# Layer 0's x read a second time, laid out by feature, and normalised with statistics sent through memory

## The chip, the cores and the metric

The kernel runs on one core of one Trainium2 chip. The metric is device microseconds of one execution. Three runs of the kernel before took 1642.39, 1643.19 and 1645.04 us, so the median is 1643.19 us.

The engines go by their short names: PE is TensorE, PEld its weight load, DVE is VectorE, ACT is ScalarE, POOL is GpSimd, SP is SyncE. SP computes nothing here; it issues DMAs, strictly in the order of its queue.

## The reference

Two transformer layers on `x` of 2 x 2048 tokens with 512 features, f32 throughout:

```python
x = x + L0_xattn(layernorm(x), ctx, ctx, pad, ...)   # 16 heads of 64, RoPE, tanh cap at 30, causal, own layer norm (g, b) inside
x = x + L0_ffn(layernorm(x), ...)                    # fake-quantised SwiGLU, 1408 wide
x = x + L1_xattn(layernorm(x), ctx, ctx, mask, ...)  # 16 heads of 32, biases
x = x + L1_ffn(layernorm(x), ...)                    # top-1 of 8 experts
```

The change touches the first line and the keys and values of the third. In the first line the query input is a layer norm of a layer norm: `q = layer_norm(layernorm(x), g, b) @ Wq`. For each token a mean and one combined factor (the power -1/2 of `var*(1+EPS) + EPS*EPS`) are enough, followed by a scale `g` and a shift `b` for each feature. In the third line the context `ctx` (2 x 128 x 512) is multiplied by `Wk` and `Wv` without a norm.

## The kernel before, in words

**Residency.** `x` stays in SBUF as 32 tiles `xs[n]` of 128 tokens x 512 features, tokens on the partitions. A matmul on PE contracts over partitions, so the query projection needs x by feature (features on partitions): `xnT[k]`, 128 x 4 x 256.

**Layer 0's attention** works in 16 blocks `k` of 256 tokens (two tiles; batch alternates from block to block), and in each block on 4 groups `g` of 4 heads. A unit is `u = 4k + g`; there are 64. The order of PE, DVE and ACT is written out by hand in a loop over `u` (with `tc.manual_schedule`). POOL's and SP's orders are not written out: a scheduler places their instructions. An iteration of the loop does, on PE in this order:

- `scores(u)`: keys times queries, 16 matmuls (`sc<-q`), then ACT takes a tanh and an exponential of them;
- `queries(u + 2, 0)`: 8 matmuls (`pq<-xnT,wq`), of which DVE makes two rope products `rt[0]`, `rt[1]`;
- `mixed(u - 1)`: probabilities times values (`sc<-pr`), then DVE's reciprocal (L410) and weighting `att` (L411);
- `queries(u + 2, 1)`: 8 more matmuls, products `rt[2]`, `rt[3]` on DVE, and POOL joins them to `q` (L372, L374). So a `q` is made two units ahead of the `scores` that read it. There is one set of `rt` buffers, so the next unit's first products wait for POOL to have read the last ones;
- `projected(u - 2, t)`: 8 matmuls into `pw`.

Two things more hang on the group number.

- **The norm.** At `g == 2` of block k, `normed(k + 2)` takes the statistics of block k+2's two tiles on DVE (`variance`, `ve`) and the power on POOL (L327, `rr`); `centered(k + 2)` then subtracts the mean and multiplies by the factor on DVE (L103, `xn<-x,mv,rr`, tokens on partitions, so both are per-partition scalars). At the end of iterations `g == 0` and `g == 1`, `turned(k + 1, c0)` turns half of the block each: 4 PE transposes (L345, `pt<-ident,xn`) and 2 ACT instructions that apply `g` and `b` while they copy from PSUM into `xnT` (L347). `queries` of the next block read `xnT` from `g == 2` on.
- **The weights of the FFN.** At `g == 0` and `g == 3` a weight slice `w_in` is quantised on DVE (L271 to L277) and sent through a DMA transpose; the next slice is loaded meanwhile (`w_in` has 2 buffers).

Block 0 is normed and turned ahead of the loop, among the keys and values of the context; block 1 is centered there and turned at u = 0 and u = 1. In the blocks 0 and 1 POOL also applies the causal mask to the probabilities (L392).

**Start.** SP issues all loads in one order: weights of the keys, two tiles of x, weights of the values and queries, two tiles of x, rope tables, `wo` (2 MB), the rest of x. The last 23 tiles of x (`homes`) hold weights and context first, and are loaded when these have been read.

**Layer 1's keys** come after layer 0's attention. The context is loaded by token (`cx0`, `cx1`, on ACT's queue), turned on PE (8 transposes, `pt<-ident,cx`), copied by ACT into `ctxT` (L624), and `keys(f)` multiply it (L628). Beside them DVE finishes the last block and finds the largest |x|, which PE turns (`pm`, L590); from it comes the quantisation step of the FFN.

**Memory round trip that is there already.** `v_dram` is written by one DMA (L700) and read back, sent to all partitions, into `rowadd`; POOL then adds it to `wgate` (L703).

Of the kernel before, what the change touches and what calls it, by code (L numbers as in the profile page):

```python
# [11 lines left out]
F32 = mybir.dt.float32  # L12
# [5 lines left out]
AF = mybir.ActivationFunctionType  # L18
ALU = mybir.AluOpType
# [4 lines left out]
P = 128  # L24
B, S, T, D = 2, 2048, 128, 512
ND = D // P
# [27 lines left out]
B0 = 256  # L54
NB0 = B0 // P
# [7 lines left out]
def two_layers(ctx: ExitStack, tc: tile.TileContext, a, out):  # L63
    nc = tc.nc
# [5 lines left out]
    small = ctx.enter_context(tc.tile_pool(name="small", bufs=4))  # L70
    dram = ctx.enter_context(tc.tile_pool(name="dram", bufs=1, space=DRAM))

    def load(dst, src):
        nc.sync.dma_start(out=dst, in_=src)
# [11 lines left out]
    xs = [x[:, :D] for x in xw]  # L86
# [15 lines left out]
    def center(dst, x, mean, scale):  # L102
        nc.vector.tensor_scalar(dst, x, mean, scale, ALU.subtract, ALU.mult)  # L103
# [7 lines left out]
    def transposed(psum, src, n=ND):  # L111

        pt = psum.tile([P, n, P], F32, name="pt", tag="m")
        for c in range(n):
            nc.tensor.transpose(pt[:, c, :], src[:, c * P : (c + 1) * P], ident)
        return pt
# [33 lines left out]
    with ExitStack() as l0:  # L150
# [40 lines left out]
                wk[g].append(w.rearrange("p (c o f) -> p c o f", c=2, o=2))  # L191
        for n in order[:NB0]:
            load(xs[n], x_in[n])
        for c in range(ND):
            wv.append([])
            for f in range(E0 // D):
                w = xs[homes[8 + 2 * c + f]]
                load(w, a["L0_xattn_Wv"][c * P : (c + 1) * P, f * D : (f + 1) * D])
                wv[c].append(w)
# [6 lines left out]
        def tables_in(j):  # L206
            tabs[j] = []
            for name in ("rope_cos", "rope_sin"):
                tab = mid.tile([P, B0], F32, name=name)
                load(tab, a[name][:, j * B0 : (j + 1) * B0])  # L210
                tabs[j].append(tab)

        tables_in(0)
        load(wo, a["L0_xattn_Wo"].rearrange("(c p) f -> p c f", p=P))
        for n in order[2 * NB0 : -23]:
            load(xs[n], x_in[n])
# [62 lines left out]


        def gate_up_in(name, i):
            w = wtmp.tile([P, D], F32, name="w_in", tag="w_in")
            load(w, a[name][i * P : (i + 1) * P, :])
            return w

# [26 lines left out]
        blocks = [(j, b) for j in range(S // B0) for b in range(B)]  # L312
        tiles = [[b * TPB + j * NB0 + t for t in range(NB0)] for j, b in blocks]
        nu = len(blocks) * NG
        norms, xns, xnTs, ropes, qs, prs, atts, pws = {}, {}, {}, {}, {}, {}, {}, {}

        sc = pss.tile([P, 4, 512], F32, name="sc")

        def normed(k):


            for t, n in enumerate(tiles[k]):
                mv = variance(xs[n])
                ve = small.tile([P, 1], F32, name="ve")
                nc.vector.tensor_scalar(ve, mv[:, 1:2], 1.0 + EPS, EPS * EPS, ALU.mult, ALU.add)
                rr = small.tile([P, 1], F32, name="rr")
                nc.gpsimd.tensor_tensor(rr, ve, minus_half, ALU.pow)  # L327
                norms[k, t] = mv, rr

        def centered(k):  # L330
            xns[k] = []
            for t, n in enumerate(tiles[k]):
                mv, rr = norms[k, t]
                xn = mid.tile([P, D], F32, name="xn")
                center(xn, xs[n], mv[:, 0:1], rr)
                xns[k].append(xn)

        def turned(k, c0):

            if c0 == 0:  # L340
                xnTs[k] = mid.tile([P, ND, B0], F32, name="xnT")
            pt = psm.tile([P, 2, B0], F32, name="pt", tag="m")
            for c in range(2):
                for t, xn in enumerate(xns[k]):
                    nc.tensor.transpose(pt[:, c, t * P : (t + 1) * P], xn[:, (c0 + c) * P : (c0 + c + 1) * P], ident)  # L345
            for c in range(2):
                nc.scalar.activation(  # L347
                    xnTs[k][:, c0 + c, :], pt[:, c, :], AF.Identity,
                    bias=lnb[:, c0 + c : c0 + c + 1], scale=lng[:, c0 + c : c0 + c + 1],
                )  # L350

        def queries(u, par):
# [86 lines left out]
        def steps_along(j):  # L439

            dg = wtmp.tile([P, P], F32, name="dg", bufs=1)
            nc.vector.tensor_scalar(dg, ident, sd[:, j : j + 1], None, ALU.mult)

            def rest():
                pd = psm.tile([P, P], F32, name="pdg", tag="m")
                nc.tensor.matmul(pd, ones, dg, start=True, stop=True)
                nc.scalar.copy(sdb[:, j * P : (j + 1) * P], pd)

            return rest
# [6 lines left out]
        with tc.manual_schedule(engines={E.PE, E.DVE, E.Activation}):  # L456
            context()
            for g in range(NG):
                keys(g)
                if g == 1:  # L460
                    normed(0)
                if g == 2:
                    centered(0)
            nc.vector.tensor_scalar(pad, padu, -1e30, None, ALU.mult)
            for c in range(0, ND, 2):
                turned(0, c)
            values(0, 0)
            values(0, 1)
            queries(0, 0)
            values(1, 0)  # L470
            normed(1)
            queries(0, 1)
            values(1, 1)
            for n in homes:
                load(xs[n], x_in[n])
            queries(1, 0)
            centered(1)
            queries(1, 1)
            for u in range(nu + 2):
                k, g = divmod(u, NG)  # L480
                if u < nu:
                    scores(u)
                if u + 2 < nu:
                    queries(u + 2, 0)
                elif 1 < u < nu:
                    projected(u - 2, 0)
                if 0 < u <= nu:
                    mixed(u - 1)
                if u + 2 < nu:
                    queries(u + 2, 1)  # L490
                if u > 1:
                    for t in range(0 if u + 2 < nu or u >= nu else 1, NB0):
                        projected(u - 2, t)
                if g < 2 and k + 1 < nblk:
                    turned(k + 1, 2 * g)
                if u in turns:
                    turns[u]()
                if u in diags:
                    diags[u]()
                if g == 1 and k > 0:  # L500
                    for t in range(NB0):
                        finished(k - 1, t)
                    largest(k - 1, 0)
                if g == 2:
                    if k > 0:
                        largest(k - 1, 1)
                    if k + 2 < nblk:
                        normed(k + 2)
                        centered(k + 2)
                if g in (0, NG - 1) and u > 1:  # L510
                    if makes and not loaded:
                        load_, args, _, _ = makes[0]
                        loaded.append(load_(*args))
                    elif makes:
                        _, _, make, args = makes.pop(0)
                        turns[u + 1] = make(loaded.pop(), *args)
                        if makes:
                            load_, args, _, _ = makes[0]
                            loaded.append(load_(*args))
                if nu - 5 <= u < nu - 1:  # L520
                    diags[u + 1] = steps_along(u - nu + 5)
                if u == NG:
                    for name, clip in clips.items():
                        kept[name] = const.tile([P, 1], F32, name=f"kept_{name}")
                        nc.scalar.activation(kept[name], clip, AF.Exp, scale=-1.0)
                        nc.vector.tensor_scalar(kept[name], kept[name], 1.0, None, ALU.add)
                        nc.vector.reciprocal(kept[name], kept[name])
                if u == nu - 2:
                    load(wk1, a["L1_xattn_WkT"].rearrange("(c p) f -> p c f", p=P))
                    load(wv1, a["L1_xattn_WvT"].rearrange("(c p) f -> p c f", p=P))  # L530
            largest(nblk - 1, 1)
# [67 lines left out]
    with ExitStack() as up:  # L599
# [3 lines left out]
        kv = up.enter_context(tc.tile_pool(name="kv1", bufs=1, reuse_waits="tile"))  # L603

        ctxT = kv.tile([P, ND, B * T], F32, name="ctxT")
        cxs = [kv.tile([P, D], F32, name=f"cx{b}") for b in range(B)]
        bk = kv.tile([P, ND], F32, name="bk")
        bvb = kv.tile([P, D], F32, name="bvb")

        for b in range(B):  # L610
            nc.scalar.dma_start(out=cxs[b], in_=a["ctx_1024"][b])
        nc.scalar.dma_start(out=bk, in_=a["L1_xattn_bk"].rearrange("(c p) -> p c", p=P))
        load(bvb, a["L1_xattn_bv"].partition_broadcast(P))
        load(wq1, a["L1_xattn_WqT"].rearrange("(c p) f -> p c f", p=P))
# [4 lines left out]
        load(masks, a["mask_scores"].rearrange("(j p) k -> p j k", p=P))  # L619


        for b in range(B):
            pt = transposed(psm, cxs[b])
            nc.scalar.copy(ctxT[:, :, b * T : (b + 1) * T], pt)  # L624
        def keys(f):
            pk = psm.tile([P, B * T], F32, name="pk", tag="m")
            for c in range(ND):
# [656 lines left out]
```

## Time and profile before

| | us |
|---|---|
| median of 3 runs | 1643.19 (1642.39 to 1645.04) |
| the profiled execution: its own time | 1642.48 |
| its span in the profile | 1640.8 |
| PE busy | 1597.7 (97%) |
| DVE busy | 1185.9 (72%) |
| ACT busy | 686.3 (42%) |
| POOL busy | 437.5 (27%) |

The granted PE clock is 0.998 over the span. A row of the groups has the line, engine, operation, written and read tiles, shape and count; then busy time, mean duration of one in ns, idle time of the engine ahead of it and what ended that. In a timeline a row is a run of like instructions: start, duration in us, what, and in brackets the idle time before it. In the table of windows each engine has its busy time in us and its count of instructions, and the last three columns are the granted clock, the share of time that the DMA engines were busy, and GB/s. The page's chain of work that ended last holds only the last 8 us of this kernel, and so says nothing of layer 0; the windows and the timelines do.

### The profile page before, as it was taken

To read this page: it belongs to the slowest core of one execution; us is meant where nothing else is said; L and a number is where in the kernel's file an instruction comes from. 1 tells how busy PE (TensorE), PEld (TensorE's weight loads), DVE (VectorE), ACT (ScalarE), POOL (GpSimd) and SP (SyncE) were. 2 spreads that over 40 slices of the span, in tenths; PEclk is the share of its full clock that TensorE was granted. 3 is DMA by queue.
4 is the path that set the end of the run, shared out by engine and by line. 5 is a ranking of instruction groups with operands and counts; after the bars stand their busy time and mean duration, and the time that the engine had idled before them with its cause. 6 is when DMAs were issued, how large, how long until landed. Compare 5 with 4: busy or idle time off the path is not lost. (4 is left out here: it accounts for less than half of the span.)

```text
span 1640.8 us, 26515 instructions
## 1 busy us (share of the span) xinstructions
PE 1597.7 (97%) x9962; PEld 952.5 (58%) x9962; DVE 1185.9 (72%) x2290; ACT 686.3 (42%) x1539; POOL 437.5 (27%) x498
## 2 busy tenths in 40 slices
PE   7999999999999999989999999999999999999997
PEld 5666666665666666534443566666666666654543
DVE  3466666777777765689986678898999889876332
ACT  1222222222222222234436576666666665662332
POOL 2322222222222221110005632333333221224553
PEclk9999999999999999999999999999999999999999
DMA  9400111010100220556658650001000000113332
GB/s 318 151 17 22 28 26 27 20 27 20 27 20 14 54 37 1 161 161 183 186 175 294 235 204 16 27 20 33 21 27 20 21 14 21 40 47 103 125 124 67
DMA packets 123883, 128.61 MB, mean 78 GB/s; under 512 B 43857, under 2 KB 91433, under 8 KB 123756
## 3 DMA queue, kind: packets, MB, share of 16 engines
q1 hardware_dynamic: 114508, 107.03, 21.2%
q0 software_dynamic: 6240, 18.70, 3.6%
q8 instruction: 80, 1.31, 0.3%
q10 hardware_dynamic: 3008, 1.19, 0.3%
q14 instruction: 47, 0.39, 0.1%
HBM read 78.96 MB, written 41.76 MB: 74 GB/s over the span
## 5 line engine op out<-in xcount | busy, mean ns | idle before, releaser
L362 PE MATMUL pq<-xnT,wq 128*128 128x256 f32 x1024 | 254.4, 392 | 0.0
L420 PE MATMUL pw<-wo,att 128*128 128x512 f32 x512 | 230.9, 593 | 0.0
L362 PEld LDWEIGHTS pq<-xnT,wq 128*128 128x128 f32 x1024 | 184.6, 190 | 66.9 <-issue 46.7
L855 ACT ACTIVATE s<-s,mx 128x128 f32<-128x128 f32 x512 | 176.7, 387 | 18.1 <-DVE mx L846 18.1
L388 ACT ACTIVATE pr<-sc 128x1024 f32<-128x1024 f32 x64 | 65.5, 1024 | 237.8 <-PE sc L383 234.7
L372 POOL TENSOR_TENSOR q<-rt,rt 128x256 f32<-128x256 f32 x64 | 46.5, 726 | 410.5 <-DVE rt L371 410.5
L420 PEld LDWEIGHTS pw<-wo,att 128*128 128x128 f32 x512 | 97.0, 190 | 96.2 <-issue 89.8
L410 DVE RECIPROCAL rd<-sc 128x256 f32<-128x256 f32 x64 | 112.5, 1757 | 51.1 <-PE sc L404 51.1
L1119 PE MATMUL pz<-we,x 128*128 x312 | 140.7, 594 | 0.6 <-issue 0.5
L813 PE MATMUL pq<-xT,wq 128*128 128x256 f32 x512 | 124.1, 385 | 0.0
L347 ACT ACTIVATE xnT<-pt,lnb,lng 128x256 f32<-128x256 f32 x64 | 32.6, 559 | 216.1 <-PE pt L345 216.1
L367 DVE TENSOR_TENSOR rt<-pq,rope_cos 128x256 f32<-128x256 f32 x64 | 27.2, 425 | 130.8 <-PE pq L362 120.2
L905 PE MATMUL pw<-wo,oT 128*128 128x512 f32 x256 | 115.5, 594 | 1.6 <-DVE oT L897 1.6
L928 PE MATMUL pl<-wgate,xnT 128*128 128x512 f32 x256 | 115.1, 592 | 0.0
L813 PEld LDWEIGHTS pq<-xT,wq 128*128 128x128 f32 x512 | 94.9, 190 | 28.0 <-issue 13.6
L716 ACT ACTIVATE gate<-pg,gsc 128x512 f32<-128x512 f32 x88 | 60.5, 687 | 96.5 <-PE pg L711 85.8
L711 PE MATMUL pu<-xqT,wuT 128*128 128x512 bf16 x352 | 90.3, 379 | 5.3 <-DVE h L719 5.3
L91 DVE BATCH_NORM_STATS2 st<-x 128x6 f32<-128x512 f32 x130 | 89.6, 689 | 5.6 <-DMA x<-in_ctx 3.4
L841 DVE SCALAR_TENSOR_TENSOR s<-sc,keep 128x1024 f32<-128x1024 f32 x64 | 77.9, 1217 | 20.6 <-PE sc L833 20.6
L1123 DVE TENSOR_TENSOR x<-x,x 128x512 f32<-128x512 f32 x39 | 27.0, 692 | 90.0 <-ACT x L1122 89.8
L711 PE MATMUL pg<-xqT,wgT 128*128 128x512 bf16 x352 | 90.3, 379 | 0.0
L1119 PEld LDWEIGHTS pz<-we,x 128*128 128x128 f32 x312 | 56.4, 190 | 58.2 <-issue 57.9
(218 smaller groups left out, 2847.7 us busy)
## 6 DMA issues: line engine op xcount, KB each, us to landing
h_dram<-h SPq DMA_DIRECT2D x88, 256.0 KB
hq<-h_dram SPq DMA_DIRECT2D x31, 704.0 KB
x_dram<-x SPq DMA_DIRECT2D x32, 258.0 KB
x<-in_x SPq DMA_DIRECT2D x32, 256.0 KB
we<-in_L_ffn_We SPq DMA_DIRECT2D x8, 1024.0 KB
w_in<-in_L_ffn_w_gate SPq DMA_DIRECT2D x11, 256.0 KB
w_down<-in_L_ffn_w_down SPq DMA_DIRECT2D x4, 704.0 KB
w_in<-in_L_ffn_w_up SPq DMA_DIRECT2D x11, 256.0 KB
```

Of the source, the lines that this page charges most:

```text
L91: nc.vector.bn_stats(out=st, in_=x)
L362: nc.tensor.matmul(pq, wqs[c // 2][:, c % 2, par, g * P : (g + 1) * P], xnTs[k][:, c, :], start=(c == 0), stop=(c == ND - 1))
L388: nc.scalar.activation(pr, sc[:, :, :B0], AF.Tanh, scale=1.0 / (math.sqrt(DH0) * GROK))
L410: nc.vector.reciprocal(rd, sc[:, 0, B0:])
L420: nc.tensor.matmul(pw, atts[u][:, f, t * P : (t + 1) * P], wo[:, 2 * g + f, :], start=(g == 0 and f == 0), stop=(g == NG - 1 and f == 1),)
L711: nc.tensor.matmul(dst, w[:, c, i * P : (i + 1) * P], xqTs[blk][:, c, :], start=(c == 0), stop=(c == ND - 1),)
L813: nc.tensor.matmul(pq, wq1[:, c, f * P : (f + 1) * P], xTs[blk][:, c, :], start=(c == 0), stop=(c == ND - 1))
L841: nc.vector.scalar_tensor_tensor(s, sc[:, 2 * half : 2 * half + 2].rearrange("p r c k -> p (r c) k"), -MASKED, keeps[n].unsqueeze(1).to_br ...
L855: nc.scalar.activation(s[:, h, :], s[:, h, :], AF.Exp, bias=mx[:, h : h + 1], **accum)
L905: nc.tensor.matmul(pw, os_[n][:, c, :], wo1[:, c, :], start=(c == 0), stop=(c == ND - 1))
L928: nc.tensor.matmul(pl, xn2T[n][:, c, :], wgate[:, c, :], start=(c == 0), stop=(c == ND - 1))
L1119: nc.tensor.matmul(pz, ring[j][:, c, :], we[:, bass.ds(e, 1), c, :], start=(c == 0), stop=(c == ND - 1))
```

## The change

The host sends two more arrays: `x_turned`, x by feature in blocks of 256 tokens, and `ctx_turned`, the context by feature. For blocks 1 to 15 `xnT[k]` is loaded directly (512 KB, `features_in`). Its mean and factor now vary along the free dimension, so each block's statistics (`stat`, 128 x 2 x 2) go by a DMA to DRAM in pieces of 4 bytes, come back by a second DMA that sends the row of 512 numbers to all partitions (`along`), and two tensor-tensor instructions of 128 x 1024 apply them: the subtraction on POOL (`centered`), the product on DVE (`scaled`). ACT then applies `g` and `b` in place (`affine`). `normed(k + 2)` sends at `g == 2` of block k; `centered` and `scaled` of that block stand at `g == 0` of block k+1, two units later; all four `affine` instructions at `g == 1`. Block 0 goes the old way (`first_block`). `xnT` has 3 buffers instead of 2, `along` one, `w_in` one instead of two. The per-token `x` is still loaded, for the residual and the statistics.

```diff
+        def features_in(k):
+            xnTs[k] = mid.tile([P, ND, B0], F32, name="xnT", bufs=3)
+            load(xnTs[k], a["x_turned"][k // B, k % B])
...
         tables_in(0)
+        features_in(1)
         load(wo, a["L0_xattn_Wo"].rearrange("(c p) f -> p c f", p=P))
...
-            w = wtmp.tile([P, D], F32, name="w_in", tag="w_in")
+            w = wtmp.tile([P, D], F32, name="w_in", tag="w_in", bufs=1)
...
         def normed(k):
+            stats[k] = small.tile([P, NB0, 2], F32, name="stat")
             for t, n in enumerate(tiles[k]):
...
-                rr = small.tile([P, 1], F32, name="rr")
-                nc.gpsimd.tensor_tensor(rr, ve, minus_half, ALU.pow)
-                norms[k, t] = mv, rr
+                nc.vector.tensor_copy(stats[k][:, t, 0:1], mv[:, 0:1])
+                nc.gpsimd.tensor_tensor(stats[k][:, t, 1:2], ve, minus_half, ALU.pow)
+            if k > 1:
+                features_in(k)
+            if k > 0:
+                turned_in(k)
+
+        def turned_in(k):
+            nc.sync.dma_start(out=stat_dram[k].rearrange("t s p -> p (t s)"), in_=stats[k].rearrange("p t s -> p (t s)"))
+            along[k] = mid.tile([P, NB0, 2, P], F32, name="along", bufs=1)
+            load(along[k], stat_dram[k].partition_broadcast(P))
+
+        def by_token(k, i, op, engine):
+            x = xnTs[k].rearrange("p c (t q) -> p c t q", t=NB0)
+            engine.tensor_tensor(x, x, along[k][:, :, i].unsqueeze(1).to_broadcast([P, ND, NB0, P]), op)
 
         def centered(k):
...
+            by_token(k, 0, ALU.subtract, nc.gpsimd)
+
+        def scaled(k):
+            by_token(k, 1, ALU.mult, nc.vector)
...
+        def affine(k, c0, pt=None):
+            for c in range(c0, c0 + 2):
                 nc.scalar.activation(
-                    xnTs[k][:, c0 + c, :], pt[:, c, :], AF.Identity,
+                    xnTs[k][:, c, :], xnTs[k][:, c, :] if pt is None else pt[:, c - c0, :], AF.Identity, bias=lnb[:, c : c + 1], scale=lng[:, c : c + 1]
                 )
...
                 if u < nu:
                     scores(u)
+                if g == 0 and k + 1 < nblk:
+                    centered(k + 1)
...
-                if g < 2 and k + 1 < nblk:
-                    turned(k + 1, 2 * g)
+                if g == 1 and k + 1 < nblk:
+                    for c in range(0, ND, 2):
+                        affine(k + 1, c)
...
                         normed(k + 2)
-                        centered(k + 2)
...
+                if g == 0 and k + 1 < nblk:
+                    scaled(k + 1)
...
-        for b in range(B):
-            nc.scalar.dma_start(out=cxs[b], in_=a["ctx_1024"][b])
+        nc.scalar.dma_start(out=ctxT, in_=a["ctx_turned"])
...
-        for b in range(B):
-            pt = transposed(psm, cxs[b])
-            nc.scalar.copy(ctxT[:, :, b * T : (b + 1) * T], pt)
```

In the built program the changed parts stand so on the queues that the scheduler fills. On SP, for each block in the middle of the stage: the load of `xnT` of block k+1, the write of block k's `stat`, the load of its `along`, then `w_in` and the DMA transpose of the group's weights, twice. On POOL, for each block: the two powers of `normed`, straight after them `centered` of the same block (not two units later, where the loop calls it), and then the `q` of `g == 3`, `g == 0` and `g == 1`. The first product of the following unit on DVE (`rt[0]`) now waits for POOL. In block 0 one mask (that of u = 3) stands behind `centered(2)`. At the start `stat(1)` is written between the loads of the `homes` on SP, with three more loads between it and `along(1)`.

More of the change, by code (lines that the diff above doesn't have):

```diff
@@ L193, in two_layers @@
             load(xs[n], x_in[n])
+        xnTs = {}
+        def features_in(k):
+            xnTs[k] = mid.tile([P, ND, B0], F32, name="xnT", bufs=3)
+            load(xnTs[k], a["x_turned"][k // B, k % B])
         for c in range(ND):
@@ L314, in two_layers @@
         nu = len(blocks) * NG
-        norms, xns, xnTs, ropes, qs, prs, atts, pws = {}, {}, {}, {}, {}, {}, {}, {}
+        stats, along, ropes, qs, prs, atts, pws = {}, {}, {}, {}, {}, {}, {}
+        stat_dram = dram.tile([len(blocks), NB0, 2, P], F32, name="stat_dram")
         sc = pss.tile([P, 4, 512], F32, name="sc")
         def normed(k):
+            stats[k] = small.tile([P, NB0, 2], F32, name="stat")
             for t, n in enumerate(tiles[k]):
@@ L325, in normed @@
                 nc.vector.tensor_scalar(ve, mv[:, 1:2], 1.0 + EPS, EPS * EPS, ALU.mult, ALU.add)
-                rr = small.tile([P, 1], F32, name="rr")
-                nc.gpsimd.tensor_tensor(rr, ve, minus_half, ALU.pow)
-                norms[k, t] = mv, rr
-        def centered(k):
[L331 to L346, printed above, removed]
+                nc.vector.tensor_copy(stats[k][:, t, 0:1], mv[:, 0:1])
+                nc.gpsimd.tensor_tensor(stats[k][:, t, 1:2], ve, minus_half, ALU.pow)
@@ new lines, in centered, with first_block, rest @@
+        def centered(k):
+            by_token(k, 0, ALU.subtract, nc.gpsimd)
+        def scaled(k):
+            by_token(k, 1, ALU.mult, nc.vector)
+        def first_block():
+            xn = mid.tile([P, NB0, D], F32, name="xn", tag="xnT", bufs=3)
+            for t, n in enumerate(tiles[0]):
+                center(xn[:, t, :], xs[n], stats[0][:, t, 0:1], stats[0][:, t, 1:2])
+            xnTs[0] = mid.tile([P, ND, B0], F32, name="xnT", bufs=3)
+            def rest():
+                for c0 in range(0, ND, 2):
+                    pt = psm.tile([P, 2, B0], F32, name="pt", tag="m")
+                    for c in range(2):
+                        for t in range(NB0):
+                            nc.tensor.transpose(
+                                pt[:, c, t * P : (t + 1) * P], xn[:, t, (c0 + c) * P : (c0 + c + 1) * P], ident
+                            )
+                    affine(0, c0, pt)
+            return rest
@@ L347, in turned @@
+        def affine(k, c0, pt=None):
+            for c in range(c0, c0 + 2):
                 nc.scalar.activation(
-                    xnTs[k][:, c0 + c, :], pt[:, c, :], AF.Identity,
-                    bias=lnb[:, c0 + c : c0 + c + 1], scale=lng[:, c0 + c : c0 + c + 1],
+                    xnTs[k][:, c, :], xnTs[k][:, c, :] if pt is None else pt[:, c - c0, :], AF.Identity, bias=lnb[:, c : c + 1], scale=lng[:, c : c + 1]
                 )
@@ L462, in two_layers @@
                 if g == 2:
-                    centered(0)
+                    first = first_block()
             nc.vector.tensor_scalar(pad, padu, -1e30, None, ALU.mult)
-            for c in range(0, ND, 2):
-                turned(0, c)
+            first()
             values(0, 0)
@@ L476, in two_layers @@
             queries(1, 0)
-            centered(1)
             queries(1, 1)
@@ L605, in two_layers @@
         ctxT = kv.tile([P, ND, B * T], F32, name="ctxT")
-        cxs = [kv.tile([P, D], F32, name=f"cx{b}") for b in range(B)]
         bk = kv.tile([P, ND], F32, name="bk")
         bvb = kv.tile([P, D], F32, name="bvb")
-        for b in range(B):
-            nc.scalar.dma_start(out=cxs[b], in_=a["ctx_1024"][b])
+        nc.scalar.dma_start(out=ctxT, in_=a["ctx_turned"])
         nc.scalar.dma_start(out=bk, in_=a["L1_xattn_bk"].rearrange("(c p) -> p c", p=P))
@@ L1254 @@
     arrays["mask_pad"] = arrays.pop("mask_BxS2_bf0")
+    arrays["x_turned"] = arrays["x"].reshape(B, S // B0, B0, ND, P).transpose(1, 0, 4, 3, 2)
+    arrays["ctx_turned"] = arrays["ctx_1024"].reshape(B * T, ND, P).transpose(2, 1, 0)
     arrays["mask_scores"] = arrays.pop("mask_1x1xSxS2_bk0").reshape(S, T)
```

## Prediction

> **What bounds the kernel now.** I read the table of windows first, because the change lies in layer 0 and a share over the whole span hides a stage. Columns: window, us, then PE, PEld, DVE, ACT, POOL busy with counts, granted clock, DMA share, GB/s.
>
> ```profile
> 0.00:41.00 41.00, 31.00 (x111) 22.48 (x112) 16.28 (x49) 5.99 (x11) 9.31 (x19) 1.00 0.90 318
> 287.00:369.00 82.00, 82.00 (x541) 50.13 (x538) 57.93 (x113) 21.46 (x24) 16.98 (x24) 1.00 0.11 23
> ```
>
> The start is bound by loads (DMA 0.90, PE 31 of 41 us). After that PE is busy without a gap; DVE has 58 of 82 us, POOL 17, DMA 0.11. The list of waits says the same: from 60 to 656 us PE waited once, for 0.4 us. So what leaves PE's queue here shortens the kernel, as long as nothing else becomes later than PE.
>
> Next, PE's timeline over one block (units of `g` = 2, 3, 0, 1 start at 303.03, 312.82, 322.61, 332.83; the next at 343.06):
>
> ```profile
> 303.03 0.71 PE L383 MATMUL sc<-q,kTe 32*128 32x256 f32 x8
> ...
> 312.82 0.71 PE L383 MATMUL sc<-q,kTe 32*128 32x256 f32 x8
> ...
> 322.61 0.71 PE L383 MATMUL sc<-q,kTe 32*128 32x256 f32 x8
> ...
> 332.30 0.60 PE L345 MATMUL pt<-ident,xn 128*128 128x128 f32 x4
> 332.83 0.71 PE L383 MATMUL sc<-q,kTe 32*128 32x256 f32 x8
> ...
> 342.53 0.60 PE L345 MATMUL pt<-ident,xn 128*128 128x128 f32 x4
> 343.06 0.71 PE L383 MATMUL sc<-q,kTe 32*128 32x256 f32 x8
> ```
>
> Units without transposes last 9.79 us twice, those with them 10.22 and 10.23. The price of four transposes is this difference, 0.43 to 0.44 us, not four times their duration of 273 ns: they overlap.
>
> Then POOL and DVE around the place where the new wait comes (a row's bracket is the idle time before it):
>
> ```profile
> 314.44 0.79 POOL L327 TENSOR_TENSOR rr<-ve,minus_half 128x1 f32<-128x1 f32 x1 [0.46 <-DVE ve L325]
> 320.41 0.73 POOL L372 TENSOR_TENSOR q<-rt,rt 128x256 f32<-128x256 f32 x1 [5.18 <-DVE rt L371]
> 321.10 0.72 POOL L374 TENSOR_TENSOR q<-rt,rt 128x256 f32<-128x256 f32 x1
> ```
> ```profile
> 325.79 0.42 DVE L367 TENSOR_TENSOR rt<-pq,rope_cos 128x256 f32<-128x256 f32 x1 [3.21 <-PE pq L362]
> 326.13 0.41 DVE L368 TENSOR_TENSOR rt<-pq,rope_sin 128x256 f32<-128x256 f32 x1
> 327.25 1.76 DVE L410 RECIPROCAL rd<-sc 128x256 f32<-128x256 f32 x1 [0.70 <-PE sc L404]
> 329.04 0.69 DVE L411 TENSOR_TENSOR att<-sc,rd 128x512 f32<-128x512 f32 x1
> ```
>
> POOL has 5.2 us free after the power and DVE 3.2 us before its next product.
>
> **Part 1, transposes of layer 0.** 15 blocks lose two groups of four: 15 x (10.22 + 10.23 - 2 x 9.79) = 15 x 0.87 = 13.05 us. One group gives nothing: at u = 1 no projection covers DVE, and PE waits for `att` after the transposes.
>
> ```profile
> 62.83 0.71 PE L383 MATMUL sc<-q,kTe 32*128 32x256 f32 x8 [0.41 <-DVE att L411]
> ```
>
> Take 0.43 off: **-12.6 us**.
>
> **Part 2, what DVE, ACT and POOL get instead** (all beside PE, priced at nothing while the cover holds). DVE loses two `xn` of 0.54 and 0.55 us and a wait of 0.44 behind `normed`, and gains two copies of 0.15 (as L430) and one tensor-tensor of 1024: 256 elements take 0.41, 512 take 0.69, so about 1.25. That last one stands after the quantisation of `g == 0`, which ends at 332.36, and DVE is then idle 3.66 us until 336.01: it fits with 2.4 us over. ACT's four instructions of 0.56 us move to `g == 1`, behind the exponential that ends at 336.25: done by 338.5, while `queries` read `xnT` after 344. The subtraction on POOL: 256 elements take 0.73 us and 512 take 1.27 (L1204) with little beside, or a median of 1.85 beside a busy DVE (L780). Extended to 1024 that is 2.4 or 4.1 us; I take 2.7, since DVE is half idle there. `w_in` with one buffer: its load is issued when the quantisation has read the slice (322.57) instead of at 323.85 behind the DMA transpose; the bytes of such a load had moved by 326.5, and DVE wants them at 330.31. No cost: if the load took 4 us longer, the quantisation would begin late and run into DVE's 3.66 us of idle time.
>
> The GPSIMD Engine Reference of the Trainium skill (4.1, Engine selection) speaks against the subtraction on POOL: two-input elementwise work belongs on VectorE, GpSimd being about twice as slow. The rows agree on the ratio (1.27 to 0.69 us), but on DVE it would add 1.25 us to the nearly same idle stretch; by rule or by row the sum stays the same.
>
> **Part 3, the round trip, and who waits behind it.** The built order puts the subtraction straight behind the powers on POOL, so POOL waits there for `along`, and behind it stand `q` (L372, L374), behind these DVE's next `rt`, behind that the reciprocal and `att`, and PE's next `scores` wait for `att`. On SP the read of `along` holds up only `w_in` and a transpose that are not due for 7 us. No row shows a write in 4-byte pieces to DRAM. Nearest below: a write of `h` in 512 pieces, issued at 756.43, had moved all by 758.6 (2.2 us), and the load of `w_in` took 2.6 (323.85 to 326.5): 4.8 us. Above: a round trip amid traffic,
>
> ```profile
> 705.38 0.50 SPq L700 DMA_DIRECT2D v_dram<-vrow  x1
> ...
> 707.01 0.50 SPq L74 DMA_DIRECT2D rowadd<-v_dram  x1
> ```
> ```profile
> 711.22 2.68 POOL L703 TENSOR_TENSOR wgate<-wgate,rowadd 128x512 f32<-128x512 f32 x2 [21.75 <-DMA h_dram<-h]
> ```
>
> which is 5.8 us from write to use. I take 5.2, nearer the quiet end as DMA is 0.11 here. Then, on the old clock: power done 315.2, `along` there at 320.4, subtraction done at 323.1, both `q` (1.45) at 324.6, and `rt` wants POOL's reads done by 326.1. Slack 1.5 us. After that the delay eats DVE's 0.70 idle, then the distance from `att` (ends 329.73) to `scores` (332.83, less 0.43 for the transposes gone): 2.7. PE stalls only from 4.9 us later than reckoned, a trip plus subtraction of 12.8 us against 7.9. Cost of part 3: 0.
>
> The page DMA: Bandwidth & Descriptors (Specifications; Anatomy of one DMA) warns of exactly this write: below 512 B a read-modify-write, and about 2 us fixed for every DMA, mostly the receipt, longest in HBM. By its figure two DMAs make an estimate of 4 to 5 us, inside my range.
>
> In block 0, `centered(2)` stands before the mask of u = 3, which is read at 85.41. Power done at 73.4, plus 7.9, plus 0.64: 82.0. Covered by 3.4 us.
>
> **Part 4, start.** `features_in(1)` puts 0.5 MB ahead of `wo`: SP issues nine loads of 256 KB from 36.55 on in 5.6 us, one per 0.66, so 1.3 us later for `wo` (wanted at 69) and the rest. `stat(1)` can go at 41.9, behind 4 to 5 loads in flight (3 us): down at 46; `along` behind three more loads at about 49.4; subtraction to 52.1, `q` of u = 1 to 53.6, where `scores(1)` wants it at 55.1 and DVE's `rt` at 53.9. Just covered; a subtraction of 4.1 us or a longer queue would cost 0 to 3. I take **+0.3**.
>
> **Part 5, layer 1.** The context's transposes and copies stand between PE's last `pw` and the keys:
>
> ```profile
> 685.81 1.04 PE L115 MATMUL pt<-ident,cx 128*128 128x128 f32 x8
> 687.65 0.70 PE L628 MATMUL pk<-ctxT,wq 128*128 128x256 f32 x2 [0.80 <-ACT ctxT L624]
> ```
>
> The keys can start 1.84 us earlier; the load of `ctxT` goes out some 9 us ahead, as `cx0` did. But `pm` needs DVE's maximum, ready at 690.97, so PE will wait there. What passes is the later half: third and fourth key, then the turned x that ACT copies until 698.3. Between 0 and 1.84, I take **-0.7**.
>
> **Sum:** -12.6 - 0.7 + 0.3 = -13.0 us. From the profiled execution's 1642.48 that gives 1629.5, from the median of 1643.19 (0.7 higher) 1630.2; forecast **1629.8**.
>
> **Rivals.** (a) The gain is eaten in part: the trip or the subtraction is long enough that PE stalls at the start (up to 3 us) or by a few tenths in each block (15 x 0.3 = 4.5). For it: slack at the start is nearly nothing. Against: 4.9 us of it in the middle. 1633 to 1638. (b) Slower: the 4-byte write takes so long that trip plus subtraction passes 12.8 us; each further us stalls PE in 15 blocks. To be slower than before by more than 0.2% (3.3 us, about what a measurement of this kernel can tell from no change) it has to reach 12.8 + 16.3 / 15 = 13.9. With the long subtraction of 4.1 that is a trip of 9.8 us. At 15 us in all: 15 x 2.2 = 33 us, so 1663. For it: no row shows such a write. Against: 512 pieces in 2.2 us. (c) The saving is given back elsewhere: DVE, at 71% and with the product added, sets the pace at `g == 0`. It would have to slip 2.7 us there, and it is idle for 3.66: 1640 to 1644.
>
> **How the numbers follow.** Forecast 0.73 (1627 to 1632), (a) 0.11, (b) 0.11, (c) 0.05. Faster is forecast and (a): 0.84; same is (c): 0.05; slower is (b): 0.11. The range leaves out (b) and (c): from 1627 (all 1.84 of part 5, all 13.05, against the fastest run) to 1638.
>
> **What would show it.** Right: units of 9.79 us for every `g`, no `pt` of L345's kind after block 0, POOL's subtraction at 2.4 to 4.1 us ending before DVE's next `rt`, PE waiting nowhere between 65 and 640 us. Wrong: a PE row `sc` with idle time put down to `att`, once per block; DVE's first `rt` waiting for POOL by more than 3 us; or units at `g == 0` still over 10 us.

## The result, and the profile after

The changed kernel takes 1700.55 us (median of 4 runs, 1697.83 to 1702.2), beside 1643.36 us for the kernel before on the same chip: a ratio of 1.0352 (95% interval 1.0339 to 1.0365). It is 57 us slower; 13.4 us less were forecast. The profiled execution took 1697.83 us with a span of 1696.1.

The list of PE's waits names the place at once. Columns: what PE waited for, us in total, times, longest.

```profile
PE sc L415 <- DVE att L443: 42.4, 15, 3.8
...
PE sc L436 <- POOL pr L424: 4.3, 1, 4.3
PE sc L415 <- POOL q L404: 3.0, 1, 3.0
```

The first row, `att` once per block, is what the prediction had named as the sign of an error; 13 of these 15 waits last 2.58 to 3.84 us, one in each of the blocks 2 to 14. The other two, the mask of u = 3 and the `scores` of u = 1, are places where it had counted on just enough slack. Before, PE waited 0.4 us in all of that stretch.

The window of four blocks' work that was 82.00 us of PE without a gap now reads (same columns as before):

```profile
287.00:369.00 82.00, 75.90 (x476) 45.22 (x465) 51.27 (x101) 19.31 (x22) 18.52 (x23) 0.96 0.13 34
```

PE is busy 75.90 of 82, and a second number is new: the granted clock is 0.96 in place of 1.00.

One block shows the chain. SP's timeline, then POOL's, DVE's and PE's (the bracket is the idle time before the row and what ended it):

```profile
295.23 0.38 SPq L345 DMA_DIRECT2D stat_dram<-stat  x1
305.03 0.33 SPq L74 DMA_DIRECT2D along<-stat_dram  x1
```
```profile
294.64 0.55 POOL L337 TENSOR_TENSOR stat<-ve,minus_half 128x1 f32<-128x1 f32 x1 [0.52 <-DVE stat L336]
308.89 2.35 POOL L351 TENSOR_TENSOR xnT<-xnT,along 128x1024 f32<-128x1024 f32 x1 [13.70 <-DMA along<-stat_dram]
311.20 0.73 POOL L404 TENSOR_TENSOR q<-rt,rt 128x256 f32<-128x256 f32 x1
```
```profile
311.96 0.42 DVE L399 TENSOR_TENSOR rt<-pq,rope_cos 128x256 f32<-128x256 f32 x1 [9.26 <-POOL q L404]
```
```profile
302.75 0.71 PE L415 MATMUL sc<-q,kTe 32*128 32x256 f32 x8
...
315.61 0.71 PE L415 MATMUL sc<-q,kTe 32*128 32x256 f32 x8 [3.00 <-DVE att L443]
316.98 3.34 PE L394 MATMUL pq<-xnT,wq 128*128 128x256 f32 x8
```

A write has landed when its end is reported to SP, which then issues the read of `along` that waits for it (SP's list of waits puts these waits down to the write, 15 times). So SP's two rows time the write: 9.8 us here. Over the 15 blocks it is 8.1 to 10.6 us from issue to landing (median 8.35), though of the 528 packets of this one 495 had moved within 1.4 us and the last within 2.7. From the read's issue to the start of the subtraction it takes 3.9 to 6.4 more (median 5.2), so the trip is 13.2 to 14.7 us long. POOL stands idle for 13.70 us with `q` behind it, DVE for 9.26, and PE for 3.00. The last row shows what comes after: eight matmuls of `pq`, elsewhere 1.99 us, take 3.34. The table of windows gives the reason (us, PE busy, then the other engines, granted clock, DMA share, GB/s):

```profile
312.60:315.60 3.00, 0.01 (x1) 0.03 (x1) 2.92 (x4) 0.00 (x0) 0.01 (x1) 1.00 0.00 0
317.00:318.00 1.00, 1.00 (x6) 0.82 (x4) 0.93 (x4) 0.91 (x1) 0.34 (x1) 0.50 0.05 16
318.00:319.00 1.00, 1.00 (x4) 0.82 (x3) 1.00 (x2) 0.97 (x2) 0.00 (x0) 0.50 0.00 0
```

After these 3 us of idleness PE runs at half its clock for some 3 us (0.50 from 316.6 to 319.5). Units (from the start of one `sc<-q` to the next) last 9.79 us at `g` = 2 and 3, as forecast. At `g` = 0 they last 12.4 to 13.7 us from the third block on, and at `g` = 1 they last 11.4 us in 10 of 14 blocks and 9.79 in the others.

### The profile page after: what moved, and what is told of

Read it like the earlier page. It is cut to its first block, busy times and chain, and to the rows that moved or that the text cites. A ratio compares the mean times of both kernels' runs of the same rounds, so it can differ in the third digit from the quotient of the medians.

```text
span 1696.1 us, 26396 instructions
## 1 busy us (share of the span) xinstructions
PE 1603.6 (95%) x9810; PEld 949.3 (56%) x9834; DVE 1186.6 (70%) x2307; ACT 685.2 (40%) x1537; POOL 470.7 (28%) x513
## 5 line engine op out<-in xcount | busy, mean ns | idle before, releaser
L394 PE MATMUL pq<-xnT,wq 128*128 128x256 f32 x1024 | 269.1, 408 | 0.0
L394 PEld LDWEIGHTS pq<-xnT,wq 128*128 128x128 f32 x1024 | 194.4, 200 | 73.1 <-issue 46.3
L351 POOL TENSOR_TENSOR xnT<-xnT,along 128x1024 f32<-128x1024 f32 x15 | 35.1, 2343 | 201.4 <-DMA along<-stat_dram 201.4
L100 POOL TENSOR_TENSOR x<-ve,minus_half 128x1 f32<-128x1 f32 x32 | 17.6, 549 | 264.4 <-DVE ve L99 264.4
```

The costliest lines, as they stand in the source:

```text
L394: nc.tensor.matmul(pq, wqs[c // 2][:, c % 2, par, g * P : (g + 1) * P], xnTs[k][:, c, :], start=(c == 0), stop=(c == ND - 1))
```

## The experiments

Two theories stood against each other. Theory W: the write lands late, and POOL waits for it with `q` in its queue. Rival D: the subtraction beside DVE, or the trip's traffic, slows the block wherever it stands.

**Only POOL's order.** One word is added, so that POOL follows the order of the code; the subtraction moves behind the two `q` of the unit before.

```diff
-        with tc.manual_schedule(engines={E.PE, E.DVE, E.Activation}):
+        with tc.manual_schedule(engines={E.PE, E.DVE, E.Activation, E.Pool}):
```

> Only POOL's order is changed: it is written out as for the other engines, so that the subtraction stands where the code calls it, behind the two q of the unit before, and not straight behind the powers. The write and the read stay as they are. Theory W (the write of 4-byte pieces lands after 8 to 10 us, and it costs only because POOL waits for it with q behind): along lands some 5 us into the unit of g = 0, the subtraction is done at about 8 and both q at 9 to 9.5, just before they are wanted; PE no longer waits for att once per block, all units return to 9.79 us, and the time falls to about 1630 (1628 to 1645, the upper end if q comes a few tenths late). Rival D (it is the subtraction beside DVE, or the traffic of the round trip, that slows the block, not the place of the wait): above 1690, as with the whole change.

Measured: 1634.62 us (1634.15 to 1634.7), 0.9953 of the kernel before (0.9937 to 0.997), which took 1641.47 us beside it. The write is as slow as ever (8.4 to 10.9 us), yet every unit from u = 3 to the last block has 9.79 us. POOL still waits, but nothing that is due stands behind it:

```profile
290.16 2.36 POOL L351 TENSOR_TENSOR xnT<-xnT,along 128x1024 f32<-128x1024 f32 x1 [7.29 <-DMA along<-stat_dram]
292.48 0.72 POOL L404 TENSOR_TENSOR q<-rt,rt 128x256 f32<-128x256 f32 x1
```

What is left is at the start, where the subtraction for block 1 still waits for its trip ahead of a `q`: PE waits once for 4.0 us, and u = 1 and u = 2 last 10.40 and 12.44 us, beside 7.27 and 9.79 before. Theory W holds; from u = 3 on the traffic and the subtraction alone cost nothing that shows.

**Pieces of 16 bytes.** Each partition's four numbers lie together in memory; 128 pieces in place of 512. POOL's order stays as built.

```diff
-        stat_dram = dram.tile([len(blocks), NB0, 2, P], F32, name="stat_dram")
+        stat_dram = dram.tile([len(blocks), P, NB0, 2], F32, name="stat_dram")
...
-            nc.sync.dma_start(out=stat_dram[k].rearrange("t s p -> p (t s)"), in_=stats[k].rearrange("p t s -> p (t s)"))
+            nc.sync.dma_start(out=stat_dram[k], in_=stats[k])
...
-            engine.tensor_tensor(x, x, along[k][:, :, i].unsqueeze(1).to_broadcast([P, ND, NB0, P]), op)
+            engine.tensor_tensor(x, x, along[k][:, :, :, i].rearrange("p q t -> p t q").unsqueeze(1).to_broadcast([P, ND, NB0, P]), op)
```

> POOL's built order is as in the changed kernel, but the statistics lie in memory token by token, so that each partition writes one piece of 16 bytes: 128 pieces in place of 512 of 4 bytes; by_token reads along with a stride of four elements. Theory W1 (the landing time goes with the number of pieces): the write lands in 3 to 4 us, the trip with the subtraction takes about 11, below the 12.8 us from which PE stalls, and the time is 1630 to 1640. Theory W2 (any write in pieces this small takes 8 us to be acknowledged): the write still takes 8 us or more and the time stays at 1690 to 1702. A strided read that makes the subtraction and the product longer (each by up to 1 us) would show in their rows.

Measured: 1627.85 us in one run, then in five more:

> The 16-byte version again, timed against the kernel before. From the one look (1627.85) and the units of 9.79 us: 1627 to 1631, ratio 0.990 to 0.994.

1630.86 us (1630.05 to 1631.82) beside 1643.37, a ratio of 0.9923 (0.991 to 0.9937). In the profiled one of these the write lands in 1.4 us in 11 of 15 blocks, faster than theory W1 had it, and in 2.3 to 3.7 us in the others. SP's timeline of this run, and POOL's in a block whose write took 3.7 us:

```profile
310.11 0.33 SPq L345 DMA_DIRECT2D stat_dram<-stat  x1
311.51 0.33 SPq L74 DMA_DIRECT2D along<-stat_dram  x1
```
```profile
277.84 2.88 POOL L351 TENSOR_TENSOR xnT<-xnT,along 128x1024 f32<-128x1024 f32 x1 [6.93 <-DMA along<-stat_dram]
```

The price of the strided read is there, a mean of 2.87 us for the subtraction in place of 2.34 and of 2.11 for DVE's product in place of 1.28, and it is hidden: all units from u = 2 to the last block have 9.79 us.

**No trip at all**, the transposes gone as in the change.

```diff
-            if k > 0:
-                turned_in(k)
...
-                if g == 0 and k + 1 < nblk:
-                    centered(k + 1)
...
-                if g == 0 and k + 1 < nblk:
-                    scaled(k + 1)
```

> The transposes are gone as in the change, and the round trip, the subtraction and the product are left out with them (so layer 0's x of blocks 1 to 15 is not normalised; the statistics are still computed, x still comes in by feature and ACT still applies weight and bias). This is what the change would be worth with a free round trip. By parts 1, 4 and 5 of the prediction: 1629 to 1631. If it lands above 1634, something other than the round trip (the loads at the start, layer 1, the one buffer of w_in) takes time too, and then the loss of 57 us is not the trip's alone.

Measured: 1631.01 us (1629.2 to 1631.61), a ratio of 0.9933 (0.9917 to 0.995). Nothing else in the change costs time that these runs can tell (some 2 us), and the 16-byte version is as fast as one that has no trip.

**The subtraction on DVE**, straight ahead of the product.

```diff
-            by_token(k, 0, ALU.subtract, nc.gpsimd)
+            by_token(k, 0, ALU.subtract, nc.vector)
...
-                if g == 0 and k + 1 < nblk:
-                    centered(k + 1)
...
                 if g == 0 and k + 1 < nblk:
+                    centered(k + 1)
                     scaled(k + 1)
```

> The subtraction goes to DVE, straight ahead of the product at the end of g = 0, where DVE's order is written; POOL never waits for the round trip. Both theories on the trip's length leave it at 13 to 14.5 us, so along is there about 5 us into the unit of g = 0, before DVE reaches the place. Theory W: no engine waits for the trip, DVE has 2.5 us for the two operations in an idle stretch of 3.66, PE does not stall, 1629 to 1634. Rival D (DVE becomes the bound at g = 0 with the two operations): units of g = 0 or g = 1 above 10 us, the time 1640 to 1660.

Measured: 1630.36 us (1629.14 to 1631.52), a ratio of 0.9931 (0.9914 to 0.9947). The write is as slow as in the change (8.4 to 11.4 us) and hurts nobody: all units from u = 2 to the last block have 9.79 us. Both operations together take 2.48 us and leave DVE 0.82 us of idle time:

```profile
325.76 2.48 DVE L351 TENSOR_TENSOR xnT<-xnT,along 128x1024 f32<-128x1024 f32 x2
329.06 0.42 DVE L399 TENSOR_TENSOR rt<-pq,rope_cos 128x256 f32<-128x256 f32 x1 [0.82 <-PE pq L394]
```

**PE kept busy in its wait**, to weigh the clock's share.

```diff
+                if g == 1 and 0 < k < nblk - 1:
+                    for _ in range(3):
+                        nc.tensor.matmul(pws[k - 1, 0], zeros, wo[:, 0, :], start=False, stop=False)
                 if u < nu:
                     scores(u)
```

> The whole change, and ahead of the stalled scores at g = 1 of blocks 1 to 14 three matmuls of a zero matrix into the sum of pw that is open there (they add nothing). The round trip, the order on POOL and the 3 us until att comes stay; PE is busy in most of them. Theory: the second loss, units of g = 1 at 11.43 in place of 9.79 us, comes from the lower clock that PE gets after 3 us of idleness, so with the filler these units return to 9.79 and the time falls by 11 x 1.64 = 18 us, to some 1682 (1678 to 1690), with the stalls for att shortened by the 2.7 us or so of filler. If the slow pq is caused by something else (DVE or POOL late, or traffic), the units stay at 11.4 and the time at 1697 to 1702 or above.

Measured: 1702.14 us (1700.76 to 1703.71), a ratio of 1.0359 (1.0343 to 1.0375) to the kernel before. The time did not fall; that expectation was wrong. The units say why:

```profile
322.90 2.74 PE L515 MATMUL pw<-wo,zeros 128*128 128x512 f32 x6
327.00 0.71 PE L417 MATMUL sc<-q,kTe 32*128 32x256 f32 x8 [1.36 <-DVE att L445]
...
328.07 1.99 PE L396 MATMUL pq<-xnT,wq 128*128 128x256 f32 x8
```

`pq` is back at 1.99 us, at a granted clock of 1.00, and the units at `g` = 1 of 14 blocks sum to 138.7 us in place of 153.6, all but one at 9.79 (in that one the clock is at 0.50 again): the slow units are the clock's doing, 14.9 us of them. But in this kernel `att` comes later. Filler and wait make 4.1 us where the change waits 3.0, because the write landed in 9.1 us (median) and the read took 5.4, 1.0 us more together; the units at `g` = 0 gave back 15.1 us, and the first four units 5.8, since there the write took 10.7 us in place of 8.1. Why the same write takes 0.8 us longer here was not found.

**Both remedies**, 16 bytes and the written order.

> The 16-byte version with POOL's order written out as in the run with the order alone. If what that run lost against the run without a round trip (some 4 us, at the start and at two waits for att) came from the long trip, this one lies at 1628 to 1631 like the 16-byte version; if it came from the written order itself (the first q behind the subtraction that waits for along at u = 0), at 1632 to 1635.

Measured: 1631.32 us (1630.48 to 1634.39), a ratio of 0.9925 (0.991 to 0.994), not to be told from the 16-byte version. In the profiled execution (the slowest, 1634.39) PE waited 2.1 us once at the start and u = 2 lasted 11.43 us. The first four units sum to 34.5 us, beside 37.4 in the first experiment and 32.0 in the 16-byte version: of what the first experiment lost there, the long trip made about half in this execution and the order the other half. By the medians the trip made nearly all (1634.62, 1631.32 and 1630.86), so how it divides is not settled.

**The write by itself.** One extra write per block into a buffer of its own, then a read of one element (`back`), whose issue marks the landing. For example the form E:

```python
d = dram.tile([4, P, 16], F32, name=f"form{f}_{k}")
nc.sync.dma_start(out=d[:, :, :1].rearrange("a p e -> p a e"), in_=s.unsqueeze(2))
load(back, d[0, :1, :1])
```

> Measures the write by itself. Built on the 16-byte version; in each of 14 blocks one more write goes out at g = 1, of one of seven forms in turn, into a buffer of its own, followed by a read of one element of it, so that the read's issue on SP marks the landing (this holds SP up, so the time of the whole is no measure). Forms: A 512 pieces of 4 bytes that lie side by side in memory across partitions (as in the change); B 128 pieces of 4 bytes side by side; C 128 of 8; D 512 of 16; E 512 of 4, each in a stretch of 64 bytes of its own; F 512 of 8 side by side; G 4 of 512 bytes. If the number of pieces decides, A, D, E and F take some 8 us and B, C, G 1.5 to 2.5. If it is the 4-byte size, A, B and E are slow alike, D fast. If it is neighbours in one stretch of memory that wait for one another, A and B are slow in proportion to their number (8 and 2 to 3 us), E is fast, and F lies between.

The forms D, F and G went out among the loads at the start, so they say nothing here. (The whole took 1644.93 us in its one run, with SP held up.) SP's timeline for one write of the others: A (313.70), B (358.39), C (398.76) and E (478.52):

```profile
313.70 0.43 SPq L343 DMA_DIRECT2D form<-stat  x1
...
325.08 0.24 SPq L74 DMA_DIRECT2D back<-form  x1
...
358.39 0.33 SPq L343 DMA_DIRECT2D form<-stat  x1
...
366.60 0.24 SPq L74 DMA_DIRECT2D back<-form  x1
...
398.76 0.33 SPq L343 DMA_DIRECT2D form<-stat  x1
...
401.77 0.25 SPq L74 DMA_DIRECT2D back<-form  x1
...
478.52 0.43 SPq L343 DMA_DIRECT2D form<-stat  x1
...
481.88 3.27 SPq L74 DMA_DIRECT2D back<-form  x3
```

A took 11.4 us (the other time 9.5), B 8.2 (8.9), C 3.0 (3.2), E 3.4 (3.3). B has a quarter of A's pieces and is almost as slow, so the time is not in proportion to their number, as the third alternative had it; E has all of A's pieces, as small, and is fast with 64 bytes from one to the next. So neither number nor size of the pieces decides alone; how close they lie does.

> Follows the run of the seven forms, where 128 pieces of 4 bytes side by side took 8.1 us to land, 128 of 8 took 3.0 and 512 of 4 bytes, 64 bytes apart, 3.0 to 3.3. Again one extra write in each of 14 blocks of the 16-byte version, with a read of it behind (whose issue marks the landing), at g = 1, when its source is ready (the loads at the start are over by then). Forms: H 128 pieces of 4 bytes at distances of 8 bytes; I at 16; J at 32; K at 64; L 512 pieces of 8 bytes side by side; M 512 of 16 bytes side by side; N one row-wise write of 4 pieces of 512 bytes. If pieces that share a stretch of memory wait for one another and only their number in it counts, H (as the 8-byte pieces) takes about 3 us, I about 1.5 to 2, J and K no more than 2, L 3 to 4, M 1.5 to 3, N 1.5 to 2. If the size of the piece also counts, H stays at 8 us although half as many lie in one stretch, I at 3 or more. The time of the whole, with SP held up, is no measure: some 1640.

Landing times of the two writes of each form:

| form | us |
|---|---|
| 128 x 4 bytes, 4 apart (B above) | 8.2, 8.9 |
| H: 128 x 4 bytes, 8 apart | 2.7, 2.9 |
| I: 16 apart | 1.8, 1.9 |
| J: 32 apart | 1.8, 1.4 |
| K: 64 apart | 1.7, 1.5 |
| L: 512 x 8 bytes side by side | 3.3, 5.4 |
| M: 512 x 16 bytes side by side | 3.0, 4.1 |
| N: 4 x 512 bytes (until the read's issue) | 1.5, 1.2 |

H with 4-byte pieces lands as 8-byte pieces side by side do (C: 3.0), so the size of the piece does not count by itself, and from 16 bytes of distance on little is left to gain. This is the first alternative, with two exceptions: L and M took longer than it said (3.3 and 5.4 us for 3 to 4, 3.0 and 4.1 for 1.5 to 3), and the number of pieces keeps a part (512 at 64 bytes, E, 3.3; 128, K, 1.5 to 1.7). That pieces in one stretch of memory wait for one another is not shown. A distance of 4 bytes is also the only one here at which two pieces fall into the same 8 bytes, and the forms do not separate the two readings. How long such a stretch would be they do not show either, nor what happens in memory. (In this run the whole took 1627.88 us, not some 1640: the extra writes held up nothing.)

## Why the prediction was wrong

**The step that failed** is the first term of part 3: the round trip of 5.2 us (bounds 4.8 and 5.8). It was 13.2 to 14.7 us. The write took 8.35 (median) and the read 5.2; the lower bound had 2.2 for the write, from `h` (as many pieces, 512, but of 512 bytes), and 2.6 for the read, from `w_in`. These two are times until the bytes had moved. The packets of `stat` had moved in 2.7 us too; what the sum lacked is the time from there to the landing, 7.1 us in the block shown. The prediction also counted pieces, where what counts first is how close they lie. It said that no row shows such a write, and yet set its upper bound by a row of another shape (`v_dram`, also in pieces of 512 bytes, landed in 1.6 us). A bound from rows that lack the doubtful feature is no bound on it.

**The slack was worked out rightly.** It said that PE stalls once trip plus subtraction pass 12.8 us. In the block shown, the power is done at 295.19 and the subtraction at 311.24: 16.05 us, so 3.25 us of stall; measured 3.00. In the kernel with the filler it is 16.98 us, so 4.2; measured 2.74 + 1.36 = 4.1. In the 16-byte version a trip plus subtraction of 9.8 us (power done at 270.91, subtraction at 280.72) stalls nothing. Two numbers of the same kind follow from the longer trip: the mask of u = 3, "covered by 3.4 us", is late by 15.78 (trip plus subtraction there) - 7.9 - 3.4 = 4.5 us, measured 4.3; and the start, between 0 and 3 us, took its upper end, 3.0.

**Rival (b) was the outcome**, with its mechanism and its place, at 0.11. Its price at 15 us in all was 15 x 2.2 us; by the same rule the 16.05 us of the block shown give 15 x 3.25 = 49 us. It did not hold the loss of the clock after most stalls, 16.5 us: the prediction put that term at nothing without a word, and it is the second thing that it lacked.

**The sum.** From the units of the profiled executions, against the 16-byte version: at `g` = 0 of 14 blocks 185.8 us for 137.1, 48.8 more; at `g` = 1 153.6 for 137.1, 16.5 more; in the first units 2.9 more. Together 68.2 us, beside 66.4 us between the spans of these two executions (1696.1 and 1629.7); the medians lie 69.7 apart (1700.55 and 1630.86).

**Part 1** was right: without stalls the units of `g` = 0 and 1 fall from 10.23 to 9.79, 14 blocks give 12.2 us, and the first block nothing (its u = 0 shorter, its u = 1 longer by 0.4); 12.6 was forecast. **Part 5** was right. From the last `pw` to the first `pg` before, and then in the 16-byte version's first run:

```profile
678.84 7.13 PE L420 MATMUL pw<-wo,att 128*128 128x512 f32 x16
...
698.73 1.02 PE L711 MATMUL pg<-xqT,wgT 128*128 128x512 bf16 x4
```
```profile
667.00 7.13 PE L452 MATMUL pw<-wo,att 128*128 128x512 f32 x16
...
679.27 0.30 PE L624 MATMUL pm<-ident,mb 128*128 128x128 f32 x1 [1.68 <-DVE bq L713]
...
686.10 1.03 PE L740 MATMUL pg<-xqT,wgT 128*128 128x512 bf16 x4
```

It is 19.10 in place of 19.89 us: 0.8 gained (forecast 0.7), the rest eaten by `pm`, as told. **Part 2** was right in its sizes: subtraction 2.34 us (2.7 taken), product a mean of 1.28 (1.25), and neither the one buffer of `w_in` nor DVE sets the pace. The forecast of 1629.8 us is close to the time of this change with a trip that fits or with none: 1630.4 to 1631.3 in four kernels.

**The rules weighed.** That two-input work belongs on VectorE (GPSIMD Engine Reference of the Trainium skill, 4.1, Engine selection) was said to leave the sum the same. With the subtraction on DVE the kernel gains 70 us on the change, but not by the operation's speed: it is as fast with the operation left on POOL and the trip shortened. What it moves is the wait, off a queue with `q` in it. The warning of DMA: Bandwidth & Descriptors (Specifications; Anatomy of one DMA) pointed at the right DMA: it names a read-modify-write below 512 bytes, without a price, and about 2 us of fixed cost, there for DMAs that GpSimd issues, while these are issued by SP. The prediction took the estimate of 4 to 5 us from the fixed cost alone (only its upper end lies inside the range of 4.8 to 5.8 that it was said to support); the pair measured 13.2 us or more. The limit of 512 bytes does not divide the slow from the fast here: pieces of 16 bytes landed in 1.4 us in most blocks, pieces of 512 bytes (N) in 1.2 and 1.5. No run shows whether a read-modify-write is what makes the 4-byte pieces slow. For the clock, TensorE: Matmul & The Clock Gate (Why this matters for your kernels) advises against idle gaps of PE above some 3 us. In the change, waits for `att` of 2.58 to 3.84 us brought the clock to 0.50 in 10 of 13 blocks, and those of 2.81, 2.82 and 2.84 us did not. So the size agrees, but 3 us is no sharp limit here: the clock also fell after 2.09 us, in the version with both remedies, and held after 3.00 us at the start of the changed kernel.

```profile
63.34 0.95 PE L415 MATMUL sc<-q,kTe 32*128 32x256 f32 x8 [2.09 <-DVE att L443]
...
65.07 2.98 PE L394 MATMUL pq<-xnT,wq 128*128 128x256 f32 x8
```
```profile
57.95 0.71 PE L415 MATMUL sc<-q,kTe 32*128 32x256 f32 x8 [3.00 <-POOL q L404]
...
59.28 1.99 PE L394 MATMUL pq<-xnT,wq 128*128 128x256 f32 x8
```

## What to carry to other kernels

Time a DMA that others wait for from its issue to its landing, not to the last byte moved. Where it has a shape that no row of the trace shows, its time is not bounded by rows of other shapes: measure that shape alone, or work out from which length it hurts and write that chance large. Send small per-partition numbers to memory so that each partition writes one piece of 16 bytes or more, and put a wait for a round trip on a queue in which nothing due stands behind it; either alone was enough here for nearly all of it. Price a stall of PE of about 3 us at its length plus the matmuls that may follow at half clock, here another 1.65 us after 10 of 13 stalls.

## What the runs showed of the hardware

A write of 2 KB to memory in 4-byte pieces that lie side by side lands 8.1 to 10.6 us after its issue in the changed kernel (median 8.35; up to 11.4 in other runs), the same 2 KB in 16-byte pieces after 1.4 us in most blocks and 2.3 to 3.7 in the others; the same number of 4-byte pieces, 64 bytes apart, after 3.3 to 3.4 us. The clock of PE fell to 0.50 for some 3 us after waits of 2.09 and 2.58 us and held after others of 2.84 and 3.00 us.
